# Layer 0 of a four-layer kernel: order of loads, place of the first shared block, mask comparison and expert weights

## The chip, the cores and the metric

The kernel runs on one core of a Trainium2 chip. A core has a matrix engine (TensorE, PE), three engines for element work (VectorE or DVE, ScalarE or ACT, GpSimd or POOL) and a sequencer for transfers (SyncE, SP); its transfers share 16 DMA engines. Each engine works through its own list of instructions in a fixed order and waits on semaphores for the others. The metric is the device time of one execution in microseconds (us); lower is better.

## The reference

Input is x (2 x 1024 x 256, float32; here 2048 tokens of 256 channels), a condition vector for each of the two sequences, a mask of 1024 x 1024 and the weights of four layers. Each layer adds the output of a conditioning block and a feed-forward block to x. Only layer 0 and one check for layer 1 matter here:

```python
x = x + L0_ffn(L0_cond(x, cond, weight), ...)      # layer 0
x = x + L1_ffn(L1_cond(x, cond, mask, ...), ...)   # layer 1
...
# L0_ffn
shared_out = silu(x @ sgw) * (x @ suw) @ sdw        # 256 -> 512 -> 256, every token
logits = x @ gate_w                                 # 32 experts
topk_ids, topk_val = argmax(logits), max(logits)
xs = x * sigmoid(topk_val)
# each token through the 256 -> 512 -> 256 gated block of its own expert
routed_out = (silu(xs @ g[e]) * (xs @ u[e])) @ d[e]
return shared_out + routed_out
```

The conditioning block of layer 0 multiplies x by a 256 x 256 weight, scaled for each sequence by the condition vector and normalised. Layer 1 masks its attention scores with the mask. The kernel has a short form of layer 1 for a mask whose rows are all equal, and a long one otherwise; it counts at run time the entries in which rows differ from the first.

## The kernel before

**Layout.** Tokens lie on columns in `XT` (x) and `HT` (x after the conditioning), 2 x 128 channels on the partitions; 2048 tokens are NT = 16 tiles of 128 or NB = 4 blocks of TB = 512. `Xt` and `Ht` hold the same with tokens on partitions. `Ht` is part of a buffer called ACC (`Hr`, 258 wide: 256 channels and two extra columns); its last tile, `k.zero`, also serves as a source of zeros until tile 15 is written. A ring of 20 pieces of 512 KB holds weights: two pieces take the conditioning weight and its products, three are held for the shared block, and fifteen remain, which is five experts of three pieces.

**Who sets the order.** The code lists instructions; a scheduler (the Tile framework) gives each engine its order and its semaphores from data dependences, buffer reuse and its own estimates. `_behind(k, inst, ref)` adds an order without a semaphore: `inst` comes after `ref` in the list. `_after` adds a real wait. SP issues almost all loads, in order, with at most eight semaphores in turn for outstanding ones.

**The stages of `_layer0`, in the order of the profile:**

1. SP loads the condition vector (2 KB), the first half of `XT` (1 MB, issued in `tile_adaln_ffn_kernel`), the conditioning weight `W` (256 KB), the gate weight, the second half of `XT`, the three shared weights (`ring<-in_L_s`), and then writes zeros to the row buffer `xbuf` (6,063 KB) and to a part of `ybuf` (2,688 KB) from `k.zero`. A memset on DVE (L411) fills the two extra columns of all 16 tiles of ACC.
2. DVE squares `W` (L417), PE forms the norm (`pd`, L421), and for each block of tokens two products `ph` (L433); ACT scales them into `HT` (L435).
3. Router: PE forms logits from `HT` (`ps_lt`, L1200) and transposes them (`l_pl`, L1210), DVE copies them to `l_lg` and finds the maximum and its index (L177, L179).
4. `_route_static` (L509): DVE makes a one-hot table (L186) and a running sum over the tiles (sixteen additions, L518); PE adds over the tokens of a tile (`R`, L520, and L522 after the running sum, `cnt`, L525); some twenty DVE operations (L527 to L567) turn this into a row number for each token (`rows`, L557).
5. PE turns each of the 16 tiles of `HT` into token order (`ps_tm`, L354), ACT scales it by the score into `Ht` (L447), and POOL scatters it to `xbuf` (L285; 128 rows each), after the zero store has landed. Then the 16 tiles of `XT` are turned and copied by DVE into `Xt` (L453).
6. Two of the four shared blocks (`_shared`, blocks 0 and 1): four steps `f`, each with products `spg` and `spu` (L1245), silu on ACT (`ssg`, L1250), a product on DVE (`sa`, L1252) and `spo` on PE (L1255). `_shared` calls `hook` after every step and hands it the last product and the last matmul. The result is added to `Xt` (L459).
7. `_layer1_pre` (L598): loads five weights of layer 1, loads the first mask row to all partitions (`m0`) and the mask in four pieces of 256 rows (`mm`), compares and counts (`l_ne`, L620; `l_dif`, L621; the sum over partitions `pd`, L625; `l_differ`, L627), then transposes (`l_pn`, L636) and small products for layer 1 (`pt`, `pu`, `pn`). `_router_biases` adds sixteen tiny products (`pb`).
8. The slots: 24 slots of 128 rows of `xbuf`, each with rows of one to three experts. `Slots.fetch` loads `xs` (L301, which waits for every scatter), PE transposes it (`ps_cm`, L363), DVE copies it to `xsT` (L1405). `Split.slot` (L1563) forms `fpg`, silu, the transposes `fpt` of the slot before, `fpu`, the product `fa` (L1576), and `fpo`; `faT` (L1552) is DVE's half of a copy of `fpt`. The weights of an expert are loaded when the code first needs them (`weights`, L464).
9. Overflow slots under run-time branches (L491), then shared blocks 2 and 3 with the gathering of the expert outputs, then layer 1, which reads `l_differ` (L2162).

Of the kernel before, what the change touches and what calls it, by code (L numbers as in the profile page):

```python
# [8 lines left out]
F32 = mybir.dt.float32  # L9
I32 = mybir.dt.int32  # L10
U32 = mybir.dt.uint32
U8 = mybir.dt.uint8
BF16 = mybir.dt.bfloat16
AF = mybir.ActivationFunctionType
ALU = mybir.AluOpType
AX = mybir.AxisListType
# [3 lines left out]
P = 128  # L20
D = 256

DR = D + 2
S = 1024
N = 2048
NT = N // P
TB = 512
NB = N // TB
# [12 lines left out]
class Ring:  # L41


    def __init__(self, t, n):
        self.t, self.n, self.i, self.held = t, n, 0, set()
# [33 lines left out]
def _bc(ap, axis, shape):  # L79
    return ap.unsqueeze(axis).to_broadcast(shape)  # L80


def _wload(nc, t, src):
    nc.sync.dma_start(t, src.rearrange("(c p) f -> p c f", p=P))
# [184 lines left out]
class Rows:  # L269
# [30 lines left out]
    def load(self, dst, src):  # L300
        i = self.k.nc.sync.dma_start(dst, src)  # L301
        _after(self.k, i, self.new)
        self.read.append(i.ins.name)


class Lead:
# [40 lines left out]
    return k.nc.sync.dma_start(dst.rearrange("(p r) d -> p r d", p=P), _bc(k.zero[:, 0:d], 1, [P, n, d]))  # L347


def _token_major(k, psum, src, t):  # L350

    ps = psum.tile([P, 2, P], F32, name="ps_tm", tag="t", bufs=2)
    for c in range(2):
        k.nc.tensor.transpose(ps[:, c, :], src[:, c, t * P:(t + 1) * P], k.ident)  # L354
    return ps.rearrange("p c d -> p (c d)")


# [30 lines left out]
def _layer0(k):  # L388
# [6 lines left out]
    with ExitStack() as ctx:  # L395
# [6 lines left out]
        W2, Wb1 = k.ring.take().rearrange("p (n c f) -> n p c f", n=2, c=2)  # L402
        _wload(nc, W, A["L0_cond_weight"])
        gw = rp.tile([P, 2, E], F32, name="l0_gw")
        _wload(nc, gw, A["L0_gate_w"])
        _wload(nc, XT[:, :, S:N], A["xT"][:, S:N])
        hold = []
        shw = _shared_weights(k, "L0_s1", "L0_s3", "L0_s2", F, hold)
        k.x = Rows(k, xbuf, [_zero_rows(k, xbuf)])
        k.t = Rows(k, k.tbuf, [])  # L410
        nc.vector.memset(k.Hr[:, :, D:], NONE)  # L411
        _zero_rows(k, ybuf[NS * T:(NS + NOV) * T, :])
        ys = rp.tile([P, 2, 2], F32, name="l0_ys")
        nc.vector.tensor_scalar_mul(ys, k.cT, 1.0 / 16.0)
# [26 lines left out]
        m8, ixf = _top(nc, rp, lg, E, "l0")  # L441
        score = rp.tile([P, NT], F32, name="l0_score")
        nc.scalar.activation(score, m8[:, :, 0], AF.Sigmoid)
        k.x.begin()
        rows, eid, nov = _route_static(k, rp, psum, ixf, E, C, NOV, "l0")
        for t in range(NT):
            nc.scalar.activation(Ht[:, t, :], _token_major(k, psum, HT, t), AF.Copy,  # L447
                                 scale=score[:, t:t + 1])
            k.x.scatter(k.Hr[:, t, :], rows[:, t:t + 1])


        for t in range(NT):
            nc.vector.tensor_copy(Xt[:, t, :], _token_major(k, psum, XT, t))  # L453

        def shared(tb, hook=None):
            po = _shared(k, pool, psum, HT, tb, *shw, hook)
            for i in range(2):
                t = tb * 4 + i * 2
                nc.vector.tensor_tensor(Xt[:, t:t + 2, :], po[i], Xt[:, t:t + 2, :], ALU.add)  # L459

        def weights(src):
            ws = [k.ring.take().rearrange("p (c f) -> p c f", f=f) for f in (F, F, D)]
            for w, n in zip(ws, ("L0_r1", "L0_r3", "L0_r2")):
                nc.sync.dma_start(w, A[n][src].rearrange("o (c p) f -> p (o c) f", p=P))  # L464
            return ws

        for tb in range(2):
            shared(tb)
        _layer1_pre(k, k.pre, psum)
        _router_biases(k, psum)  # L470

        ws = {}
        slots = Slots(k, pool, psum)
        split = Split(k, pool, psum, slots, F)
        for i in range(NS):
            lo, cols = i * T, []
            while lo < (i + 1) * T:

                e = lo // C
                if e not in ws:  # L480
                    ws[e] = weights(slice(e, e + 1))
                n = 64 if i % 3 == 1 else 32
                cols.append((slice(lo - i * T, lo - i * T + n), ws[e]))
                lo += n
            split.slot(i, cols)
        split.finish()
        n = nc.values_load(nov[0:1, 0:1], min_val=0, max_val=NOV)

# [17 lines left out]
        c.finish()  # L506


def _route_static(k, pool, psum, ixf, E, C, nov, name):  # L509


    nc = k.nc
# [4 lines left out]
    for t in range(NT):  # L517
        nc.vector.tensor_add(cum[:, t + 1, :], cum[:, t, :], oh[:, t, :])  # L518
    R = psum.tile([P, NT, E], F32, name=name + "_R", tag="mm")
    nc.tensor.matmul(R.rearrange("p t e -> p (t e)"), k.before,  # L520
                     oh.rearrange("p t e -> p (t e)"), start=True, stop=False)
    nc.tensor.matmul(R.rearrange("p t e -> p (t e)"), k.ones,  # L522
                     cum[:, 0:NT, :].rearrange("p t e -> p (t e)"), start=False, stop=True)
    cnt = psum.tile([P, E], F32, name=name + "_cnt", tag="mm")
# [70 lines left out]
    return r.rearrange("n i p e c f -> p n i e c f"), o  # L595


def _layer1_pre(k, pp, psum):  # L598

    nc, A = k.nc, k.A  # L600
# [3 lines left out]
        _wload(nc, w[n], A["L1_W" + n])  # L604
    with ExitStack() as ctx:
        pool = ctx.enter_context(tc_pool(k, "l1pr", 1))

        m0 = pool.tile([P, S], U8, name="l1_m0")
        nc.sync.dma_start(m0, A["mask"][0:1, :].to_broadcast([P, S]))

        k.mh = pp.tile([P, TB], U8, name="l1_mh")
        for g in range(4):
            q = slice(32 * g, 32 * g + 32)
            nc.gpsimd.tensor_copy(k.mh[q, :], m0[q, (g % 2) * TB:(g % 2 + 1) * TB])
        dif = pool.tile([P, 8], F32, name="l1_dif")
        for i in range(4):
            mm = pool.tile([P, 2, S], U8, name="l1_mm", bufs=2)
            nc.sync.dma_start(mm, A["mask"][i * 256:(i + 1) * 256].rearrange("(t p) s -> p t s", p=P))
            ne = pool.tile([P, 2, S], U8, name="l1_ne", tag="l1_big")
            nc.vector.tensor_tensor(ne, mm, _bc(m0, 1, [P, 2, S]), ALU.not_equal)  # L620
            nc.vector.tensor_reduce(dif[:, 2 * i:2 * i + 2], ne, AX.X, ALU.add)  # L621
        d1 = pool.tile([P, 1], F32, name="l1_d1")
        nc.vector.tensor_reduce(d1, dif, AX.X, ALU.add)
        pd = psum.tile([P, 1], F32, name="l1_pd", tag="t", bufs=2)
        nc.tensor.matmul(pd, k.ones, d1, start=True, stop=True)  # L625
        k.differ = pp.tile([P, 1], I32, name="l1_differ")
        nc.vector.tensor_copy(k.differ, pd)  # L627

        nat = {}
        for n in ("q", "k"):  # L630
# [754 lines left out]
class Slots:  # L1385

    def __init__(self, k, pool, psum, of=None, base=0):
        self.k, self.pool, self.psum, self.of, self.base = k, pool, psum, of, base  # L1390
        self.xs, self.dst = {}, {}

    def fetch(self, i):

        if i not in self.xs:
            self.xs[i] = self.pool.tile([P, DR], F32, name="xs", bufs=4)
            self.k.x.load(self.xs[i], self.k.xbuf[i * P:(i + 1) * P, :])

    def rows(self, i, made=None):

# [122 lines left out]
class Split:  # L1523
# [42 lines left out]
    def slot(self, i, cols):  # L1566
        nc, pool = self.k.nc, self.pool
        xT = self.slots.rows(i)
        pg = self.product("fpg", xT, cols, 0)
        sg = pool.tile([P, self.F], F32, name="fsg", tag="sg")  # L1570
        nc.scalar.activation(sg, pg, AF.Silu)
        if self.old:
            aT = self.turn(self.old[1])
        pu = self.product("fpu", xT, cols, 1)
        a = pool.tile([P, self.F], F32, name="fa", tag="sa")
        nc.vector.tensor_mul(a, sg, pu)  # L1576
        if self.old:
            self.end(self.old[0], aT, self.old[2])
        self.old = i, a, cols

    def finish(self):
        i, a, cols = self.old
# [546 lines left out]
def kernel(ctx: ExitStack, tc: tile.TileContext, A, out):  # L2129
# [17 lines left out]
    k.Ht = k.Hr[:, :, 0:D]  # L2147
    k.zero = k.Hr[:, NT - 1, :]
    _consts(k)
    _wload(nc, k.XT[:, :, 0:S], A["xT"][:, 0:S])  # L2150
    dp = ctx.enter_context(tc.tile_pool(name="rows", bufs=1, space=DRAM))
    k.xbuf = dp.tile([47 * P, DR], F32, name="xbuf")

# [106 lines left out]
```

## Time and profile before

| what | us |
|---|---|
| median of 3 runs (lowest, highest) | 1567.14 (1563.42, 1574.32) |
| the profiled execution, its own time | 1562.23 |
| its span | 1560.5 |
| PE busy in the span | 1465.7 |
| DVE, ACT, POOL busy | 477.3, 303.6, 285.4 |
| first matmul starts | 9.76 |
| first scatter issued; last one issued | 56.25; 79.62 |
| first row load `xs` issued | 84.04 |
| first transpose of a slot (`ps_cm`) | 110.89 |
| first matmul of a slot (`fpg`) | 112.10 |
| last output of a slot copied (`ys`) | 273.32 |

Times inside the kernel count from the start of the span. A line of the timeline reads: start, duration, engine, source line, operation, output<-input, shape, count; in square brackets the idle time of that engine just before, and the work that ended it. "PEld" is the load of the stationary operand, which overlaps matmuls; "SPq" is SP's issue of a transfer, not the transfer. A float32 matmul of 512 columns shows as two records. The mean granted TensorE clock over the span is 0.967 of full speed. The table of stretches gives, for each, its length and the busy time of each engine with the number of instructions.

### The profile page before, as it was taken

How to read it: one execution, taken by the hardware profiler on the slowest of the kernel's cores; microseconds unless marked ns; L12 is line 12 of the kernel's file. 1: busy time of each engine (PE TensorE's matmuls, PEld its weight loads, DVE VectorE, ACT ScalarE, POOL GpSimd, SP SyncE). 2: the span in 40 equal slices, each digit the busy share in tenths (PEclk: the TensorE clock that was granted, in tenths of full speed). 3: DMA queues.
4: the chain of work that ended last, by engine and by line, in shares of the span. 5: the costliest groups of instructions: out<-in, count | busy, mean ns of one | idle time of the engine just before them, and what ended most of it. 6: DMA issues, size and time to landing. Idle time of an engine off the chain costs nothing. (4 is left out here: it accounts for less than half of the span.)

```text
span 1560.5 us, 23587 instructions
## 1 busy us (share of the span) xinstructions
PE 1465.7 (94%) x8602; PEld 1019.3 (65%) x8602; DVE 477.3 (31%) x1591; ACT 303.6 (19%) x641; POOL 285.4 (18%) x317
## 2 busy tenths in 40 slices
PE   6879999976999999999999999999999999998897
PEld 2543333433555787555599999999995558864675
DVE  3732222223411354341121111111113514456432
ACT  2312221112111212111111111111111212125222
POOL 0410000300132242023101011010110073410342
PEclk9879999987999999999999999999999999998799
DMA  9759995813211286051142434354607257672470
GB/s 249 268 187 322 342 350 191 273 57 122 75 48 55 73 275 205 28 196 48 41 138 79 175 121 150 127 181 160 207 15 258 97 187 251 214 222 70 145 248 21
DMA packets 184243, 252.48 MB, mean 162 GB/s; under 512 B 17111, under 2 KB 137823, under 8 KB 184112
## 3 DMA queue, kind: packets, MB, share of 16 engines
q1 hardware_dynamic: 164448, 210.92, 41.3%
q0 software_dynamic: 14176, 36.63, 6.5%
q10 hardware_dynamic: 5488, 3.25, 0.7%
q8 instruction: 74, 1.21, 0.3%
q14 instruction: 57, 0.47, 0.1%
HBM read 284.86 MB, written 50.76 MB: 215 GB/s over the span
## 5 line engine op out<-in xcount | busy, mean ns | idle before, releaser
L1255 PE MATMUL spo<-ring,sa 128*128 128x256 f32 x768 | 191.9, 392 | 13.8 <-DVE sa L1252 13.8
L285 POOL DMA_INDIRECT tbuf<-ys,sdst x114 | 112.2, 984 | 506.7 <-ACT ys L1517 381.9
L1255 PEld LDWEIGHTS spo<-ring,sa 128*128 128x128 f32 x768 | 140.1, 191 | 95.6 <-DVE sa L1252 75.7
L1252 DVE TENSOR_TENSOR sa<-ssg,spu 128x512 f32<-128x512 f32 x96 | 65.9, 686 | 336.7 <-PE spu L1245 329.7
L1510 DVE TENSOR_TENSOR fa<-fsg,fpu 128x512 f32<-128x512 f32 x72 | 49.5, 687 | 315.9 <-PE fpu L1505 315.9
L1505 PE MATMUL fpu<-xsT,ring 128*128 128x128 f32 x1152 | 140.4, 275 | 0.0
L1505 PE MATMUL fpg<-xsT,ring 128*128 128x128 f32 x1152 | 140.3, 275 | 0.0
L1505 PEld LDWEIGHTS fpg<-xsT,ring 128*128 128x128 f32 x1152 | 137.1, 192 | 1.8
L1505 PEld LDWEIGHTS fpu<-xsT,ring 128*128 128x128 f32 x1152 | 134.4, 192 | 0.0
L1514 PE MATMUL fpo<-ring,fa 128*128 128x256 f32 x576 | 130.3, 379 | 0.0
L1250 ACT ACTIVATE ssg<-spg 128x512 f32<-128x512 f32 x96 | 57.3, 597 | 343.2 <-PE spg L1245 333.0
L1514 PEld LDWEIGHTS fpo<-ring,fa 128*128 128x128 f32 x576 | 106.7, 190 | 13.0
L1245 PE MATMUL spg<-HT,ring 128*128 128x512 f32 x192 | 99.9, 608 | 5.3 <-PEq L491 3.1
L1245 PE MATMUL spg<-XT,ring 128*128 128x512 f32 x192 | 98.4, 604 | 4.7 <-ACT XT L911 4.7
L1245 PE MATMUL spu<-HT,ring 128*128 128x512 f32 x192 | 92.0, 600 | 0.0
L1245 PE MATMUL spu<-XT,ring 128*128 128x512 f32 x192 | 91.6, 600 | 0.0
L1481 PE MATMUL cph<-xsT,ring 128*128 128x128 f32 x624 | 83.9, 278 | 4.1 <-DMA ring<-in_L_r 1.3
L1481 PEld LDWEIGHTS cph<-xsT,ring 128*128 128x128 f32 x624 | 76.0, 192 | 8.0 <-DVE ys L1490 3.2
L1488 PE MATMUL cpo<-ring,ch 128*128 128x256 f32 x312 | 80.2, 380 | 0.8 <-ACT ch L1484 0.8
L1509 ACT ACTIVATE fsg<-fpg 128x512 f32<-128x512 f32 x72 | 43.0, 597 | 169.7 <-PE fpg L1505 169.7
L1245 PEld LDWEIGHTS spu<-XT,ring 128*128 128x128 f32 x192 | 37.0, 193 | 44.4 <-issue 43.9
L1245 PEld LDWEIGHTS spu<-HT,ring 128*128 128x128 f32 x192 | 36.7, 194 | 42.7 <-issue 42.6
(570 smaller groups left out, 1644.8 us busy)
## 6 DMA issues: line engine op xcount, KB each, us to landing
ring<-in_L_w SPq DMA_DIRECT2D x108, 1024.0 KB
ring<-in_L_r SPq DMA_DIRECT2D x96, 512.0 KB
ring<-in_L_r SPq DMA_DIRECT2D x156, 256.0 KB
xs<-xbuf SPq DMA_DIRECT2D x138, 129.0 KB
ring<-in_L_W SPq DMA_DIRECT2D x32, 512.0 KB
yt<-tbuf SPq DMA_DIRECT2D x48, 256.0 KB
xbuf<-ACC SPq DMA_DIRECT2D x1, 6063.0 KB
ring<-in_L_s SPq DMA_DIRECT2D x6, 512.0 KB
```

The source lines that it names most:

```text
L285: i = k.nc.gpsimd.indirect_dma_start(out=self.ap, out_offset=bass.IndirectOffsetOnAxis(ap=idx, axis=0), in_=rows, in_offset=None, **end)
L1245: mm = nc.tensor.matmul(ps, W[:, c, f * P:(f + 1) * P], X[:, c, cols], start=c == 0, stop=c == 1)
L1250: nc.scalar.activation(sg, pg, AF.Silu)
L1252: mul = nc.vector.tensor_mul(a, sg, pu)
L1255: mm = nc.tensor.matmul(po[g // 2][:, g % 2, :], a[:, g * P:(g + 1) * P], W2[:, f, :], start=f == 0 and g % 2 == 0, stop=f == nf - 1, skip ...
L1481: made = [nc.tensor.matmul(ph[:, f, :], R1[:, c, f * P:(f + 1) * P], xT[:, c, :], start=c == 0, stop=c == 1) for f in range(2) for c in ra ...
L1488: made = [nc.tensor.matmul(po, h[:, f, :], R2[:, f, :], start=f == 0, stop=f == 1) for f in range(2)]
L1505: made = [nc.tensor.matmul(ps[:, j, :], W[:, c, (f0 + j) * P:(f0 + j + 1) * P], xT[:, c, :], start=c == 0, stop=c == 1) for ps, W in ((pg, ...
L1509: nc.scalar.activation(sg, pg, AF.Silu)
L1510: nc.vector.tensor_mul(a[:, f0:f0 + 4, :], sg, pu)
L1514: made = [nc.tensor.matmul(po, a[:, f, :], W2[:, f, :], start=f == 0, stop=f == 4 * nh - 1) for f in range(4 * nh)]
```

## The change

Five things, all in layer 0:

- **Order of loads.** The conditioning weight is loaded first, then `XT` in four blocks of 512 tokens, then the gate weight; the shared weights follow as before. The load of the first half of `XT` leaves `tile_adaln_ffn_kernel`.
- **The memset of the extra columns** covers tiles 0 to 14 only; the last tile, the source of the zeros, has its columns set already.
- **Shared block 0 in front of the router's sums.** `_route_static`, the turning of `HT` and `XT` and the scatters are called from hooks of the shared blocks, with `_behind` on the step's last matmul: step 0 of block 0 calls the router's sums and tiles 0 to 7 of `HT`, step 1 tiles 8 to 15, steps 2 and 3 four tiles each of `XT`; each step of block 1 two more tiles of `XT`. The order in which the instructions stand now: `spg` and `spu` of step 0 come between and after the `l_pl` transposes, its `sa` stands on DVE ahead of the one-hot table, and `R` stands on PE behind its `spo`.
- **Mask rows compared within the slots.** The comparison leaves `_layer1_pre` and becomes a generator, `_mask_rows`, with eight pieces of 128 rows; slots 1, 3, ... 17 advance it. Each comparison is ordered behind the last `fa`, and the next piece is loaded into one of two buffers.
- **Expert weights ahead of rows.** The first five experts (fifteen loads of 512 KB) are issued before the slots begin, and every row load is ordered behind the last of them on SP.

```diff
         _wload(nc, W, A["L0_cond_weight"])
         gw = rp.tile([P, 2, E], F32, name="l0_gw")
+        for tb in range(NB):
+            _wload(nc, XT[:, :, tb * TB:(tb + 1) * TB], A["xT"][:, tb * TB:(tb + 1) * TB])
         _wload(nc, gw, A["L0_gate_w"])
-        _wload(nc, XT[:, :, S:N], A["xT"][:, S:N])
...
-        nc.vector.memset(k.Hr[:, :, D:], NONE)
+        nc.vector.memset(k.Hr[:, 0:NT - 1, D:], NONE)
...
-        rows, eid, nov = _route_static(k, rp, psum, ixf, E, C, NOV, "l0")
-        for t in range(NT):
-            nc.scalar.activation(Ht[:, t, :], _token_major(k, psum, HT, t), AF.Copy,
-                                 scale=score[:, t:t + 1])
-            k.x.scatter(k.Hr[:, t, :], rows[:, t:t + 1])
-        for t in range(NT):
-            nc.vector.tensor_copy(Xt[:, t, :], _token_major(k, psum, XT, t))
...
+        def stream(t, mm):
+            nc.vector.tensor_copy(Xt[:, t, :], _token_major(k, psum, XT, t, mm))
+        def lead(f, mul, mm):
+            if f == 0:
+                k.x.begin()
+                got[:] = _route_static(k, rp, psum, ixf, E, C, NOV, "l0", mm)
+            if f < 2:
+                for t in range(8 * f, 8 * f + 8):
+                    nc.scalar.activation(Ht[:, t, :], _token_major(k, psum, HT, t, mm), AF.Copy,
+                                         scale=score[:, t:t + 1])
+                    k.x.scatter(k.Hr[:, t, :], got[0][:, t:t + 1])
+            else:
+                for t in range(4 * f - 8, 4 * f - 4):
+                    stream(t, mm)
-        for tb in range(2):
-            shared(tb)
+        got = []
+        shared(0, lead)
+        rows, eid, nov = got
+        shared(1, lambda f, mul, mm: [stream(t, mm) for t in range(8 + 2 * f, 10 + 2 * f)] if f < 4 else None)
         _layer1_pre(k, k.pre, psum)
         _router_biases(k, psum)
-        ws = {}
-        slots = Slots(k, pool, psum)
+        ws = {e: weights(slice(e, e + 1)) for e in range(5)}
+        slots = Slots(k, pool, psum, ref=sent[-1])
...
+        muls = []
+        mask = _mask_rows(k, k.pre, pool, psum, muls)
         for i in range(NS):
+            if i < 18 and i % 2 == 1:
+                next(mask)
...
-            split.slot(i, cols)
+            muls.append(split.slot(i, cols))
...
+def _mask_rows(k, pp, pool, psum, muls):
+    nc, A = k.nc, k.A
+    m0 = pool.tile([P, S], U8, name="l1_m0", bufs=1)
+    nc.sync.dma_start(m0, A["mask"][0:1, :].to_broadcast([P, S]))
...
+    for i in range(8):
+        mm = pool.tile([P, S], U8, name="l1_mm", bufs=2)
+        nc.sync.dma_start(mm, A["mask"][i * P:(i + 1) * P])
+        yield
+        ne = pool.tile([P, S], U8, name="l1_ne", bufs=1)
+        _behind(k, nc.vector.tensor_tensor(ne, mm, m0, ALU.not_equal), muls[-1])
+        nc.vector.tensor_reduce(dif[:, i:i + 1], ne, AX.X, ALU.add)
+    d1 = pool.tile([P, 1], F32, name="l1_d1", bufs=1)
+    nc.vector.tensor_reduce(d1, dif, AX.X, ALU.add)
+    pd = psum.tile([P, 1], F32, name="l1_pd", tag="t", bufs=2)
+    nc.tensor.matmul(pd, k.ones, d1, start=True, stop=True)
...
+    yield
```

In `_token_major` and `_route_static` the new argument `ref` is the matmul that the transposes, and the first matmul of `R`, are ordered behind; in `Slots` it is the load that every row load is ordered behind; `sent` collects the weight loads, and `Split.slot` returns the instruction that makes `fa`.

## The prediction

> **What bounds the kernel now.** I read the shares first: TensorE (PE) is busy 1465.7 of 1560.5 us, so a gain must come from stretches where PE stands still or runs slowly. Then I cut the front of the span into windows; the columns are stretch, length, busy us of PE, of its weight loads, VectorE (DVE), ScalarE (ACT), GpSimd (POOL), then granted clock, DMA share, GB/s.
>
> ```profile
> 0.00:10.00 10.00, 0.24 (x2) 0.24 (x2) 1.83 (x12) 1.28 (x1) 2.04 (x15) 1.00 0.62 210
> ...
> 30.00:40.00 10.00, 3.94 (x10) 1.60 (x8) 8.50 (x66) 2.70 (x7) 0.00 (x0) 0.75 1.11 223
> 40.00:50.00 10.00, 6.35 (x18) 3.65 (x19) 4.45 (x14) 2.26 (x6) 0.00 (x0) 0.57 1.09 363
> ...
> 80.00:90.00 10.00, 3.86 (x13) 2.11 (x12) 2.62 (x2) 0.19 (x1) 3.03 (x5) 0.81 0.56 167
> 90.00:100.00 10.00, 9.68 (x22) 5.75 (x23) 3.35 (x5) 0.60 (x1) 0.00 (x0) 0.68 1.06 390
> ...
> 150.00:200.00 50.00, 49.03 (x450) 19.23 (x448) 11.33 (x23) 10.36 (x23) 0.00 (x0) 1.00 1.00 347
> ```
>
> Three holes lie ahead of the slots, which begin at 110.9 us; inside the slots PE is full (49.03 of 50) and DMA too (share 1.00). The timeline gives each hole its cause:
>
> ```profile
> 9.01 0.69 DVE L417 TENSOR_TENSOR ring<-ring 128x512 f32<-128x512 f32 x1 [4.22 <-DMA ring<-in_L_cond_weight]
> ...
> 43.44 0.09 DVE L411 MEMSET ACC<- 128x32 f32 x1 [4.12 <-DMA xbuf<-ACC]
> ...
> 43.65 2.07 PE L522 MATMUL l_R<-l_cum,ones 128*128 128x512 f32 x2 [3.83 <-DVE l_cum L518]
> ...
> 84.04 0.34 SPq L301 DMA_DIRECT2D xs<-xbuf  x1
> 84.47 0.38 SPq L618 DMA_DIRECT2D l_mm<-in_mask  x1
> ...
> 87.38 2.29 DVE L620 TENSOR_TENSOR l_ne<-l_mm,l_m 128x2048 uint8<-128x2048 uint8 x1 [7.43 <-DMA l_mm<-in_mask]
> ...
> 90.32 3.78 PE L1255 MATMUL spo<-ring,sa 128*128 128x256 f32 x8 [6.46 <-DVE sa L1252]
> ```
>
> (1) The first weight lands behind 1 MB of x. (2) In the router the last two additions wait on DVE behind a memset that waits for the 6 MB zero store. (3) SyncE (SP) sits in the row load L301 until all scatters have landed; the last mask rows queue behind it, DVE waits for them, and `sa` behind DVE. The last line also shows the aftermath: 3.78 us where eight such records take 1.89 (at 74.24).
>
> **What the Trainium skill says.** *TensorE: Matmul & The Clock Gate*, Part 1 (the HAM clock gate): a PE idle for a window of about 3.4 us falls to half clock and needs about as long under load to recover. The trace agrees: weight loads 0.86 us apart from 12.48 to 14.19, then 0.43; clock 0.57 in 40–50. The same page's opening table: VectorE, ScalarE and GpSimd are strict FIFOs; agrees (the 4.12 us above). *DMA: Bandwidth & Descriptors*, "Queues, rings and completion order": a ring serves its descriptors in order, and an engine takes rows of queues in turn. So row loads queue behind expert weights, while POOL's scatters share: under 364 GB/s (64–66 us) they kept being issued every 1.27 us, landing in 2.4 to 6.6.
>
> **The change, part by part.** Times are of the profiled execution, whose own time is 1562.23 us around a span of 1560.5; that is 4.9 below the median 1567.14, so the saving is taken off the median.
>
> *Loads.* The weight (0.26 MB) now leads. The windows show 0.08, 0.22, 0.22 and 0.39 MB moved in us 3–4, 4–5, 5–6, 6–7, so it is in at 4.9, and 0.8 us later announced (the old pair was in at 8.2, DVE began at 9.01): 5.7. PE starts 3.3 us sooner. The first quarter of x is in at 6.7+0.8 = 7.5, before ph starts at 8.2; later quarters follow every 1.5 us and PE needs 3.4 each. Gate and shared weights keep their place in bytes; the zero store still ends near 43.4.
>
> *Router.* l_lg was copied by 30.97; now 30.97−3.3+0.4 = 28.1, the 0.4 for the first spg matmul, put between the l_pl transposes (0.86, less 0.46 that the second pair waited anyway). Maxima and indices 4.2 → 32.3, the new `sa` 0.69 → 33.0, one-hot 1.0 and sixteen additions of 0.224 → 37.7. The memset (L411) now spares the zero row: no wait. ACT's table loads (1.28 each, one more than before) end by 30, ahead of `sa`. PE has spg and spu done at 30.1, so still 3 us idle, where it had been at work on little from 30.2 to 45.6.
>
> *PE from 33.05 on*, at full clock: shared block 0's first spo 1.7; R and cnt 1.8; 32 token transposes (now all here) at 0.215 = 6.9; its other three steps at 5.16 (eight 512-wide matmul records of 0.43, plus spo 1.72) = 15.5; block 1 20.6. Sum 46.5 → 79.6. To it: waiting for the sums (37.7 against 36.3 reached) or cold clock, 2.5 (bounds 1.4 and 3.4); ACT and DVE hand-overs 1.5 (0 to 4; not shown before, bounded by the two table loads, 2.6, and two row-copy pairs, 1.5). Block 1 ends at 83.6. Then the layer-1 preparation: its four transpose pairs, formerly partly inside block 1, now all follow. From the old chain (natq 0.37, pt 1.05, pu 1.04, pn 0.6, pb 0.7) plus 1.3 for Xt's last adds: 7.3 → 90.9. The slots start **20.0 us sooner** (110.9−90.9).
>
> *Rows and weights.* Rows were written 9.6 us after R, 1.7 of it waiting for `spu`; now R ends 38.6 (41 if cold) and rows are there at 46.6–49. All sixteen scatters took 24.3 us; 8 of 16 Ht rows are ready, the rest by 52. Last issue 72–75, landing 75–79. SP's list: five layer-1 weights, sim, gates, then fifteen expert loads (7.9 MB) ahead of the first xs. They start near 49.6, when the ybuf zeroes land, and at 300 GB/s beside the scatters are in by 76–80; eight outstanding loads let the last be issued near 66. So xs goes out at about 77 and is in by 81–83: hidden, with 8 us to spare, behind block 1. If that cover is gone, the slots wait for xs. m0, the first mask row and POOL's four copies follow, off the path.
>
> *Mask rows within the slots.* Eight pairs of 128x1024 operations; half of 2.28 and 2.27, so 2.3 us a pair, between a slot's `fa` and the next DVE work. `faT` comes 3.5 us after `fa` (130.39 to 133.90): hidden. But in two places of the order an xsT follows (263.49, 1.5 us after `fa`): 0.9 + 1.3 us, the second with d1, pd and differ. Cost **2.2 us** (0 to 5). The loads add 6×0.13 MB in the slots, 2.3 us at 347 GB/s. Before, the last expert weights were in by about 257 and used at 263.97, so 7 us of lead remain: hidden. SP waits for DVE before each further mask row; at those places it had been waiting for PE to free the ring (31.5 us in 14 waits on ps_cm alone), so I count nothing (to 4 us).
>
> Sum: −20.0 + 2.2 = −17.8; I take **−17.5**, so 1567.1−17.5 = **1550** on the median (1544.7 for a profile like this one). Bounds of the terms: front 2.7 to 3.8, clock and hand-overs −4 to +2.5, slots −5 to 0: 12 to 22 saved.
>
> **Rivals.**
> *Rows late.* Scatters share DMA with 7.9 MB now instead of five loads; paced at 2.1 us rather than 1.5 they end at 49+34 = 83, land at 88 and xs at 92 or later; at 2.5 us, 99. For it: single scatters took 2.84 and 2.40 under load. Against: the others did not. Saved 20−8−2 = 10: 1557. Chance 0.18.
> *The slots become transfer-bound.* DMA is at 1.00; if SP's six waits for DVE cost 2 us each of issue time, plus 2.3, the 7 us of lead are gone and the end slips by 7. Against: waits for the ring, not for DMA, fill SP's list. Saved 11: 1556. Chance 0.14.
> *Slower: mask rows arrive late in the slots.* A mask row queues behind up to seven weights (7×0.52 MB at 347 GB/s = 10.6 us), and DVE, in order, holds faT and xsT behind it. One is hidden up to 1.2 us late. It eats the whole 20 us only from 3.7 us late at each of eight; 1% slower needs 5.7. At 6 us each: 8×4.8 = 38, against 20: 1585. Against: each row is asked for some four slots (26 us) ahead of its comparison in the instruction order. Chance 0.05.
> *The change does not do what it says* (the scheduler leaves the order): excluded, since in the built order R stands behind block 0's first spo and fifteen weights ahead of xs.
>
> **How the numbers follow.** My forecast has 0.63: 1545–1555. With the two rivals on the same side, 12 to 5 saved, and part of the late tail, the range is 1544 to 1562. One per cent, 15.7 us, is about what a measurement of this kernel can tell from no change. The forecast lies just beyond it: of its 0.63 I give 0.55 to a saving above 15.7, and a little (0.03) for gains that the rivals leave; within 1%: 0.08 + 0.26 + 0.03 = 0.37; slower 0.05.
>
> **What would show it.** Right: L422 near 5.7; no wait in front of the memset; rows by 49; first slot matmul at 92 (112.1 before); no DVE wait for l_mm; slots as long as before (162 us, +2). Wrong: PE waiting for xs near 90; PE waiting for ring loads late in the slots; xsT behind l_ne by more than 1.5 us; cold clock over more than 4 us after 33.

## The result and the profile after

| | before | changed |
|---|---|---|
| median of 20 runs (lowest, highest), us | 1570.36 (1563.42, 1574.32) | 1576.06 (1569.74, 1584.26) |
| ratio, 95% interval | | 1.0039 (1.0024 to 1.0054) |
| the profiled execution; its span | 1562.23; 1560.5 | 1569.74; 1567.9 |
| first scatter; last one | 56.25; 79.62 | 51.86; 70.99 |
| first row load `xs` issued | 84.04 | 77.08 |
| second shared block ends (last `spo`) | 106.3 | 100.7 |
| first matmul of a slot | 112.10 | 109.89 |
| slots: from there to the end of the last `ys` | 161.6 | 167.0 |

The change costs 0.4% where 1.1% of gain was forecast. Both profiles are quick executions: the changed kernel's is the quickest of its twenty runs, and that of before, which isn't one of the twenty, lies 1.2 us below the quickest of them and 8.1 below their median.

I matched the same instruction in both traces and took the difference of its start. The last scaling into `HT` stands at +0.1 us (later), the first scatter at −4.4, the first slot at −2.2, the last `ys` at +3.2, the end of layer 0 at +4.6. Through layers 1 and 2 that stays 4.3 to 5.2; in layer 3, 7.4 are added near 1265 us and most of them given back by 1467. So the loss lies in two places of layer 0, ahead of the slots and in them, and ahead of them a gain is lost that was there at 52 us.

The stretches of the changed kernel, columns as in the prediction (length, busy us of PE, its weight loads, DVE, ACT, POOL, then clock, DMA share, GB/s), show where:

```profile
50.00:55.00 5.00, 5.00 (x25) 3.23 (x24) 1.63 (x8) 2.63 (x7) 2.53 (x3) 1.00 1.05 341
55.00:60.00 5.00, 5.00 (x26) 3.63 (x25) 1.14 (x4) 4.22 (x6) 3.78 (x5) 1.00 1.01 349
60.00:65.00 5.00, 3.11 (x11) 1.76 (x10) 1.34 (x3) 0.00 (x0) 3.78 (x5) 1.00 1.05 402
65.00:70.00 5.00, 1.76 (x9) 0.83 (x7) 0.26 (x1) 0.00 (x0) 3.78 (x5) 1.00 1.06 403
70.00:75.00 5.00, 0.00 (x0) 0.00 (x0) 0.76 (x2) 0.21 (x1) 1.65 (x2) 0.53 1.06 404
75.00:80.00 5.00, 4.26 (x8) 2.15 (x9) 1.87 (x5) 0.39 (x1) 0.00 (x0) 0.50 1.05 387
```

The hole of before at 80 to 90 us is gone and that at 30 to 50 is smaller (PE busy 16.6 of 20 us, 10.3 before). A new one has opened from 60 to 76: of the 30 us shown PE loses 10.9. No engine is busy in its place; only POOL works evenly, and DMA is full. The timeline of the changed kernel there:

```profile
63.47 1.99 PE L1285 MATMUL spo<-ring,sa 128*128 128x256 f32 x8 [1.89 <-issue]
...
65.73 1.02 PE L1275 MATMUL spg<-HT,ring 128*128 128x512 f32 x2
...
69.74 0.69 DVE L453 TENSOR_TENSOR Xt<-spo,Xt 128x512 f32<-128x512 f32 x1 [6.33 <-remote]
...
74.67 0.69 DVE L453 TENSOR_TENSOR Xt<-spo,Xt 128x512 f32<-128x512 f32 x1 [4.24 <-remote]
74.79 0.60 ACT L1280 ACTIVATE ssg<-spg 128x512 f32<-128x512 f32 x1 [15.16 <-remote]
...
75.74 0.69 PE L355 MATMUL ps_tm<-ident,XT 128*128 128x128 f32 x2 [8.98 <-DVE Xt L465]
```

`spo` is drawn as done at 65.5 and `spg` at 66.8. DVE adds the one at 69.74 and 74.67, ACT takes the other at 74.79, and PE waits for them. "remote" means that a semaphore ended the wait but no instruction shown ends just before it. The trace's list of semaphore updates names it: PE's own signal, recorded at 60.51, then 69.71, then 74.64, 74.69, 74.73 and 74.77. The matmuls whose signals came at 69.71 and 74.64 are drawn as ending at 64.60 and 65.46, so these are 5 and 9 us late. The list of updates has holes itself (1374 updates of DVE's signal for 1463 instructions that give it; every missing one would lie within 2 us after the start of an indirect DMA of POOL), but DVE's starts at 69.74 and 74.67 agree with the two that are used here. The Trainium skill (*Perfetto Trace Analysis*, "Summary: the profiler window per engine type") says that a TensorE bar closes at an estimated end and leaves the spread of the semaphore out. That agrees with this picture; whether the matmuls themselves ran late or only their signals can't be read here.

In the slots most of the loss sits between 200 and 250 us:

```profile
150.00:200.00 50.00, 48.32 (x440) 18.61 (x432) 19.99 (x29) 10.36 (x23) 0.00 (x0) 1.00 0.97 335
200.00:250.00 50.00, 45.37 (x426) 17.71 (x428) 15.59 (x27) 9.39 (x21) 0.00 (x0) 1.00 0.98 336
```

```profile
200.00:250.00 50.00, 48.71 (x451) 19.06 (x448) 11.26 (x23) 9.77 (x23) 0.00 (x0) 1.00 0.99 352
```

The first fence is the changed kernel, the second the one before from 200 to 250 us.

### The profile page after: what moved, and what is told of

Read it like the earlier page. It is cut to its first block, busy times and chain, and to the rows that moved or that the text cites. A ratio compares the mean times of both kernels' runs of the same rounds, so it can differ in the third digit from the quotient of the medians.

```text
span 1567.9 us, 23581 instructions
## 1 busy us (share of the span) xinstructions
PE 1462.2 (93%) x8599; PEld 1018.2 (65%) x8602; DVE 479.2 (31%) x1599; ACT 304.6 (19%) x642; POOL 281.2 (18%) x317
## 3 DMA queue, kind: packets, MB, share of 16 engines
q8 instruction: 74, 1.21, 0.3%
```

## The experiments

Each kernel below has several timed runs and one profile; stalls, first slots and lengths of the slots are read from that one profile.

**Theory A, the burst:** 7.9 MB of expert weights beside the scatters hold everything up. **Theory B, the order:** token transposes and scatters put into block 0's steps do. For the slots, **theory S:** the mask comparison costs them. The first four kernels undo one part of the change each, or make one part alone.

*Weights on demand*
```diff
-        ws = {e: weights(slice(e, e + 1)) for e in range(5)}
-        slots = Slots(k, pool, psum, ref=sent[-1])
+        ws = {}
+        slots = Slots(k, pool, psum)
```


> Only the fifteen expert loads go back from 'ahead of the rows' to 'as the slots ask for them' (three of them still stand ahead of the first row load). Theory A, the burst: the stall between 60 and 76 us, in which PE is busy 9 of 20 us, comes from 7.9 MB of expert weights running beside the sixteen scatters. Then it goes: the second shared block ends near 85 us (100.5 with the change), the first slot matmul comes near 95 (109.9), held there by weights that arrive only after the rows, and the time falls by 8 to 13 us against the changed kernel, to about 1565. Theory B, the order of the work itself (token transposes and scatters put into block 0's steps): the stall stays, first slot matmul near 110, time as the changed kernel's (1576) or worse.


Measured: ratio to before 1.000 (0.9988 to 1.0013). The stall is there, with three expert loads ahead instead of fifteen: 9.7 us of PE's time lost between 50 and 80 us, and first slot matmul at 107.34. Theory A has lost its main support.

*Comparison back ahead of the slots, burst kept*
```diff
+        (the block m0 ... l_differ of the kernel before, in _layer1_pre)
-        mask = _mask_rows(k, k.pre, pool, psum, muls)
-            if i < 18 and i % 2 == 1:
-                next(mask)
```


> Only the comparison of the mask rows goes back to the layer-1 preparation, ahead of the slots; the burst stays. Theory S, the comparison costs the slots: they shrink from 167.0 us (109.9 to 276.9 in the changed kernel) to the 161.6 they took before, and nothing of it returns ahead of them, since DVE has time while PE is held up: time 5 us below the changed kernel, about 1571. Rival: the slots are longer for another reason (rows or expert weights that come late): they stay at 166 to 167 us, time 1576. The stall at 60 to 76 us stays either way.


Measured: 0.9911 (0.9872 to 0.9951), a fall of 1.3% against the changed kernel, far more than expected. The slots are back at 161.6 us, as forecast. But the stall that "stays either way" is gone: 1.1 us lost, and first slot matmul at 95.60, 16.5 sooner than before. DVE had 18 us more to do in that very stretch:

```profile
60.00:65.00 5.00, 5.00 (x18) 2.83 (x18) 5.00 (x6) 1.15 (x2) 3.78 (x5) 1.00 0.94 274
65.00:70.00 5.00, 5.00 (x23) 3.29 (x22) 5.00 (x9) 0.60 (x1) 4.09 (x4) 1.00 1.06 389
70.00:75.00 5.00, 5.00 (x18) 2.81 (x17) 4.92 (x6) 0.12 (x1) 4.39 (x3) 1.00 1.05 401
75.00:80.00 5.00, 5.00 (x20) 3.20 (x19) 5.00 (x6) 0.48 (x1) 1.59 (x3) 1.00 1.07 401
```

From 65 us on DMA is as full as in the changed kernel (389 to 401 GB/s), and PE loses nothing. The burst alone is not the cause.

*Two experts ahead:* `range(5)` becomes `range(2)`.


> Two experts (six loads, 3.1 MB) ahead of the rows instead of five. Theory A: the stall shrinks with the bytes: it ends when these loads have landed, near 62 to 66 us, so 8 to 11 us of it go, and two experts are there when the slots begin: first slot matmul at 92 to 98, time 1563 to 1568, the best of the four. Theory B: as the changed kernel, 1576.


Measured: 1.0004 (0.9988 to 1.0021); 6.5 us lost, first slot at 104.08. Stalled again.

*The kernel before with the fifteen loads ahead of the rows, and nothing else*
```diff
-        ws = {}
-        slots = Slots(k, pool, psum)
+        ws = {e: weights(slice(e, e + 1)) for e in range(5)}
+        slots = Slots(k, pool, psum, ref=sent[-1])
```


> The kernel before with nothing changed but the fifteen expert loads put ahead of the first row load. Theory A: the burst now meets the scatters at 56 to 75 us there too, and PE, DVE and ACT stand still for part of it: first slot matmul 3 to 10 us later than 112.1, time 3 to 10 us above before (1573 to 1580). Theory B: no stall; rows are hidden either way, weights are in earlier, time as before or up to 5 us less (1565 to 1570).


Measured: 0.9953 (0.9934 to 0.9972): the part that I suspected is a gain by itself. Nothing lost between 50 and 80 us, first slot at 102.64.

What do the three stalled kernels (the changed one, weights on demand, two experts ahead) share that the others lack? The mask comparison is missing beside the scatters. In the kernel before (its timeline, POOL and DVE) the two meet:

```profile
58.94 0.96 POOL L285 DMA_INDIRECT xbuf<-ACC,l_rows  x1 [0.30 <-issue]
59.92 2.28 DVE L620 TENSOR_TENSOR l_ne<-l_mm,l_m 128x2048 uint8<-128x2048 uint8 x1
60.20 2.84 POOL L285 DMA_INDIRECT xbuf<-ACC,l_rows  x1 [0.30 <-ACT l_gts L667]
63.35 0.96 POOL L285 DMA_INDIRECT xbuf<-ACC,l_rows  x1 [0.30 <-ACT ssg L1250]
...
67.69 2.28 DVE L620 TENSOR_TENSOR l_ne<-l_mm,l_m 128x2048 uint8<-128x2048 uint8 x1
68.41 2.40 POOL L285 DMA_INDIRECT xbuf<-ACC,l_rows  x1 [0.30 <-issue]
71.11 0.96 POOL L285 DMA_INDIRECT xbuf<-ACC,l_rows  x1 [0.30 <-issue]
```

A scatter takes 0.96 us of POOL, but 2.84 and 2.40 where a comparison runs beside it, and ends some 0.8 to 0.9 us after the comparison. The Trainium skill (*SBUF — State Buffer*, "SBUF: two separate sides") gives a reason: DVE and GpSimd share a pair of ports as an exclusive lock, and a DVE operation with two inputs in SBUF takes it against a GpSimd operation that reads SBUF. The trace agrees: the comparison has two such inputs; beside the reduction `l_dif`, with one, scatters keep 0.96. So the comparison broke the stream of scatters into series of at most five. **Theory C, the stream:** without a break the sixteen scatters, 1.27 us apart, are what makes PE's signals late. **Rival D:** the mask rows' loads, which held up SP's list, made the difference.

*Changed kernel with byte comparisons of no use beside the scatters* (four pairs)
```diff
+        def fill(mul):
+            for i in range(2):
+                z = pool.tile([P, S], U8, name="l1_ne", bufs=1)
+                _behind(k, nc.vector.tensor_tensor(z, XT[:, 0, 0:S // 4].bitcast(U8),
+                                                   XT[:, 1, 0:S // 4].bitcast(U8), ALU.not_equal), mul)
```


> The changed kernel with four pairs of extra byte comparisons (128x1024, 1.22 us each, of XT with itself; the result is used by nothing) put on DVE behind the multiplications of the two shared blocks, where the mask comparison stood before; no load is added or moved. Theory C, the scatters' stream: with the comparison gone from there, POOL issues sixteen scatters 1.27 us apart without a pause (51.9 to 71.0), and PE's signals come late while that lasts; a byte comparison on DVE holds POOL up for 2 to 4 us (in the run with the mask ahead of the slots: scatters 2.9, 2.5 and 3.3 us apart at comparisons of 57.2, 63.5 and 71.9) and so breaks the stream. Then the stall goes though DVE has 10 us more to do: first slot matmul near 98 (109.9), time 8 to 12 us below the changed kernel's 1576, about 1566. Rival D, the mask loads: what helped was that SP's list of expert weights was held up by mask rows and their waits for DVE. Then the stall stays and DVE's added work makes it worse: 1576 to 1582.


Measured: first slot at 95.96 (109.89), 2.3 us lost instead of 10.9, by adding 10 us of work that nobody needs. In this profile rival D falls. The time follows only in part: 0.9990 (0.9969 to 1.0011). The slots took 169.0, and the profiled run (1560.48) is the second quickest of twenty, of which twelve took 1568 to 1578; whether those stalled, no trace shows.

*Changed kernel with its scatters paced*
```diff
-                    k.x.scatter(k.Hr[:, t, :], got[0][:, t:t + 1])
+                if f == 0:
+                    todo.extend(k.x.paced(k.Hr, [got[0]]))
...
+            send(2 if f == 0 else 3, mul)      # and 3 behind each mul of block 1
```


> The changed kernel with its scatters paced: two behind the first multiplication, then three behind each further one, instead of sixteen as fast as POOL issues them; the mask comparison stays in the slots, nothing is added to DVE. Theory C: the stall at 60 to 76 us goes; last scatter at 78 to 82 us, row loads at 84 to 87, first slot matmul at 95 to 98; slots 167 us as with the change; time 1562 to 1566. Rival D: pacing the scatters does nothing, or the stall moves with the burst: first slot matmul at 108 or later, 1574 to 1580.


Measured: first slot at 96.47, 2.3 us lost, 0.9971 (0.9952 to 0.9989); the profiled run (1568.34) is among the slower of its twelve. With no work added and no load moved, this is the firmer answer to rival D. The 2.3 in this kernel and the last are another thing: DVE and ACT stood behind layer 1's small loads `l_sim` and `l_gts`. The slots took 169.9, 3 more than expected.

*Changed kernel without the mask comparison* (the flag is set by a memset)


> The changed kernel without the comparison of the mask rows and without their loads (the flag that says whether rows differ is set to 0 by a memset, which is what the comparison gives for these inputs; this part of the computation is left out). It separates the two costs of moving the comparison. Theory C: block stall as in the changed kernel (first slot matmul at 108 to 110), slots back at 162 us: 5 us below the changed kernel, 1571. Rival: if the stall had to do with the mask rows' loads that follow the row loads, it is gone as well: about 1558.


Measured: stall as expected (9.9 us lost, first slot 107.84), slots 160.1; 0.9997 (0.9975 to 1.0019). The two costs of moving the comparison are separate, and this one shows the slots' share alone.

*Comparison ahead of the slots, layer 3's scatters three to a step:* `((1, 3), 4)` becomes `((1, 3), 3)`.


> The kernel with the mask comparison back ahead of the slots (1557.5, the best so far), with one more number changed: the scatters of layer 3 go out three to a step instead of four. There the profiles of five kernels of six, all but the kernel before, show PE idle for some 7 us about 12 scatters after their stream began (in the changed kernel between 1264 and 1270 us). Theory C: slower issue takes that stall away: 5 to 7 us less, about 1551. Rival: the stall there is chance or belongs to the weights loaded beside it: no change, 1557; or the rows come later and layer 3's slots start later: up to 6 us more.


Measured: 0.9952 (0.9937 to 0.9968), against 0.9911 without the edit: a miss. Between 1246 and 1299 us of before's time it lost 14.8 us where four to a step lost 7.1. There pacing cost more than a quieter stream gave; how much of it is the later rows was not separated.

*Comparison ahead, scatters paced four to a step, `l_sim` and `l_gts` loaded first*


> The kernel with the mask comparison ahead of the slots, with two more edits: scatters go out four to a shared step behind its multiplication, and layer 1's two small loads (l_sim, l_gts) are asked for ahead of its five weights, since DVE or ACT stood 3 to 6 us behind them at 52 to 59 us in several runs. Theory C: no stall at 55 to 76 us at all, last scatter by 76, first slot matmul at 92 to 95: 1553 to 1557. Rival: comparison and pacing together make the rows late (row loads after 86): slots 3 to 6 us later than with the comparison alone, 1560.


Measured: 0.9918 (0.9886 to 0.9950), 1557.18 us; 0.5 us lost, but the last scatter at 83.71 (76 expected) and first slot at 96.90 (92 to 95). The stall is gone and the rows are late; it is no better than the comparison alone.

*Comparison ahead of the slots once more*


> The kernel with the mask comparison ahead of the slots once more, since its 1557.5 rests on five runs. Theory C: 1556 to 1560, at least 10 us below before. If the five were a lucky draw: 1562 to 1565, as the kernel that shares its layer 0 and differs in layer 3's pace (1564.1) would have it.


Measured: 1556.28, ratio 0.9905 (0.9870 to 0.9939). The first value holds: some 15 us below before and 20 below the changed kernel. It beats both. This second profile of the same kernel lost 4.3 us (1.1 in the first) and began the slots at 99.91 (95.60): at 56 to 62 us DVE waited for a mask row and ACT for `l_gts`. So single profiles of one kernel differ by 4 us at the first slot.

*The kernel before without the comparison* (flag set by a memset, rows not loaded)


> The kernel before without the comparison of the mask rows and without the loads of the rows to be compared (the flag is set to 0 by a memset; this part is left out). It has neither the burst nor the moved router, only the stream of scatters that nothing on DVE breaks. Theory C: taking 18 us of work off DVE buys little or nothing, since the stall appears here too: PE idle for 8 us or more between 62 and 82, scatters 1.27 us apart, first slot matmul at 106 or later, time 1566 to 1574. Rival: the stall needs the burst or the moved steps: none here, and the 6.46 us in which PE waited for sa behind the comparison at 90 us go as well: first slot matmul at 100 to 104, time 1560 to 1564.


Measured: 1.0019 (1.0001 to 1.0038). The kernel before, with 18 us of DVE's work taken out and nothing moved, does not get faster; its stretches:

```profile
60.00:65.00 5.00, 4.87 (x24) 2.67 (x22) 3.27 (x9) 1.67 (x3) 3.78 (x5) 1.00 0.78 292
65.00:70.00 5.00, 2.83 (x10) 1.51 (x11) 1.27 (x3) 0.00 (x0) 3.78 (x5) 1.00 0.28 102
70.00:75.00 5.00, 2.77 (x7) 0.95 (x5) 0.43 (x1) 0.60 (x1) 3.78 (x5) 1.00 0.28 102
75.00:80.00 5.00, 1.72 (x4) 1.45 (x5) 0.69 (x1) 0.34 (x1) 3.42 (x6) 0.59 0.25 78
```

PE stands as in the changed kernel, 7.8 us lost, with DMA at a quarter. First slot at 114.13, later than with the comparison (112.10). This is the strongest single profile for theory C.

*Paced kernel with the comparison only where no `xsT` follows it*
```diff
+        next(mask)                              # ahead of the slots: first loads
-            if i < 18 and i % 2 == 1:
+            if i in (1, 3, 5, 7, 9, 11, 13, 17):
                 next(mask)
...
+        next(mask)                              # behind split.finish(): sum, l_pd, l_differ
```


> The paced kernel (scatters three to a step, 1566.3) with the mask comparison still in the slots, but only at places of DVE's order where no xsT follows the comparison; the sum over the rows with its matmul goes behind the last slot. Theory S, the place: what the comparison cost in the slots (9.6 us of them in the paced kernel's profile) was paid at the two places where xsT stands behind it, once as the wait and once more as half clock after it, and at a row load that came late: slots 162 to 164 us long, time 7 us below the paced kernel, 1558 to 1560. Rival: the comparison costs by its DVE time or its loads wherever it stands: slots at 168 or more, 1566.


Measured: 0.9926 (0.9908 to 0.9944), 1560.40; slots 163.7 (169.9 in the paced kernel). The work on DVE is the same and 6.2 us of the slots' length went, so that time as such is not what they cost. The edit also asks for the mask rows sooner, so the place of the comparison and the time of its loads are not told apart. 2.1 us over the 161.6 of before remain, which I didn't trace.

Still open was what of the stream does it: the instructions, the rows or the bytes. Two more, made from the stalled kernel before without the comparison; both leave out most of the rows' contents, so only layer 0 up to the slots is read, from one execution each.

*A quarter of the rows:* `k.x.scatter(k.Hr[0:32, t, :], rows[0:32, t:t + 1])`


> The kernel before without the mask comparison (which stalls between 63 and 78 us), with each of the sixteen scatters cut to the first 32 of its 128 rows: as many instructions on POOL, a quarter of the rows and of the bytes. It leaves out three quarters of the rows, so experts and all later layers work on other data; only layer 0's profile is read, up to the first slot. If the number of instructions is what counts: stall as there, 7 to 8 us of PE's time lost between 50 and 80 us. If rows or bytes count: less than 2 us lost, first slot matmul at 102 to 106 (114.1).


*A quarter of the width:* `k.Hr[:, t, 0:64]` into a dense view of `xbuf`


> The same kernel with all 128 rows in each scatter, but 64 of the 258 columns, written close together: as many instructions and rows, a quarter of the bytes. It leaves out most of what the rows hold; only layer 0's profile is read. If the rows[...] count: stall as with full rows, 7 to 8 us lost. If the bytes count: less than 2 us lost.


Measured: 11.7 and 8.3 us lost (7.8 with full rows); first slot at 121.46 and 117.34. The stretches of the kernel with a quarter of the width:

```profile
65.00:70.00 5.00, 2.73 (x15) 1.50 (x14) 1.27 (x3) 0.00 (x0) 3.78 (x5) 1.00 0.08 26
70.00:75.00 5.00, 3.99 (x10) 1.49 (x8) 0.85 (x2) 0.00 (x0) 3.78 (x5) 1.00 0.08 26
75.00:80.00 5.00, 0.00 (x0) 0.00 (x0) 0.00 (x0) 0.60 (x1) 3.66 (x5) 0.82 0.06 20
```

DMA moves 26 GB/s at a share of 0.08, and PE stands still all the same. Neither fewer bytes nor fewer rows took the stall away; of what I tried, the unbroken series of POOL's instructions is left.

All kernels with full scatters together; a series ends where two scatters are over 1.5 us apart, "lost" is 30 us less PE's busy time from 50 to 80 us:

| kernel | longest series of scatters | PE lost, us | first slot | slots, us |
|---|---|---|---|---|
| before | 5 | 0.0 | 112.10 | 161.6 |
| before, weights ahead | 5 | 0.0 | 102.64 | 161.3 |
| comparison ahead; again | 6; 9 | 1.1; 4.3 | 95.60; 99.91 | 161.6; 160.9 |
| the same, layer 3 paced | 8 | 4.0 | 99.49 | 161.0 |
| the same, paced, small loads first | 6 | 0.5 | 96.90 | 161.3 |
| changed, filler | 7 | 2.3 | 95.96 | 169.0 |
| changed, paced | 8 | 2.3 | 96.47 | 169.9 |
| changed, paced, other places | 8 | 2.6 | 98.74 | 163.7 |
| changed | 16 | 10.9 | 109.89 | 167.0 |
| weights on demand | 16 | 9.7 | 107.34 | 166.6 |
| two experts ahead | 16 | 6.5 | 104.08 | 165.6 |
| changed, no comparison | 16 | 9.9 | 107.84 | 160.1 |
| before, no comparison | 16 | 7.8 | 114.13 | 160.5 |

Not all that is lost is the stall. With the comparison ahead (all profiles but the paced one), in the filler and in the paced kernel it is waits for layer 1's small loads or a mask row at 55 to 62 us, and so are 2.7 us with weights on demand and 2.2 in the changed kernel without the comparison. That leaves 6.5 to 10.9 us for a series of sixteen. The 2.6 of the paced kernel with other places, a series of eight, is the stall on a small scale: `spg`, drawn as done at 65.35, is taken by ACT at 67.06.

## Why the prediction was wrong, step by step

**Loads: 3.3 us forecast, 1.0 and then nothing measured.** The weight was announced at 8.00, not 5.7 (9.01 before). Its 256 packets of 1 KB moved from 4.81 to 7.63 us, beside those of x from 5.5 on; my sum let it move alone from 3 us. PE then began at 8.74, 1.0 sooner than before (9.76), and the clock took that back. In the timelines of the changed kernel, then of before:

```profile
8.00 0.69 DVE L422 TENSOR_TENSOR ring<-ring 128x512 f32<-128x512 f32 x1 [3.46 <-DMA ring<-in_L_cond_weight]
...
14.88 0.34 PEld L438 LDWEIGHTS ph<-XT,ring 128*128 128x128 f32 x1 [0.52 <-issue]
15.73 0.20 PEld L438 LDWEIGHTS ph<-XT,ring 128*128 128x128 f32 x1 [0.52 <-issue]
...
16.79 0.69 ACT L440 ACTIVATE HT<-ph,l_dd 128x512 f32<-128x512 f32 x1 [1.84 <-PE ph L438]
```

```profile
14.19 0.34 PEld L433 LDWEIGHTS ph<-XT,ring 128*128 128x128 f32 x1 [0.52 <-issue]
14.79 0.19 PEld L433 LDWEIGHTS ph<-XT,ring 128*128 128x128 f32 x1 [0.26 <-issue]
```

The weight loads of `ph` stand some 0.85 us apart at half clock and 0.43 at full. The first record of full clock is at 15.73 in the changed kernel, 7.0 us after PE began, and at 14.52 before, 4.8 after. ACT only follows PE; its last scaling stands at 27.09 (27.01 before). In the kernels with this front the full clock came 4.5 to 7.8 us after PE's first matmul and the last scaling from 2.1 us sooner than before to 0.2 later. My sum had no term for that.

**Router: right in kind.** No wait in front of the memset, `R` sooner than before (42.03 against 43.65), rows at 50.80 (55.19). The forecast of 46.6 to 49 missed by the front and a cold `spo` of 3.49 us.

**PE's work from 33.05 us: the step that failed.** It is the term "ACT and DVE hand-overs 1.5 (0 to 4)". With the series of scatters whole, PE lost 10.9 us between 50 and 80 waiting for hand-overs, and the clock was at half from 70.35 to 80.59; block 1 ended at 100.7, not 83.6. (Half clock over more than 4 us after 33 was one of the signs of being wrong that the prediction had named; it had not named this cause.) With the series broken and all else as in the change block 1 ended at 86.8 and 87.3, so the rest of the sum was 3.2 to 3.7 short, 2.3 of it the waits for layer 1's small loads. I had read the comparison as a pure burden on DVE, its 6.46 us wait, and taken it out at no price. The sign of what it held up stood in my own text: "single scatters took 2.84 and 2.40 under load". These two are the scatters of 60.20 and 68.41, each beside a comparison. I put them down to DMA load, for a rival in which scatters come late. They came in time (70.99), and in one series, and the series did the harm.

**Layer-1 preparation: 7.3 forecast; 9.2 from the end of block 1 to the first slot matmul** (8.4 with the comparison ahead).

**Rows and weights: right.** Last scatter 70.99 (72 to 75 forecast), row load at 77.08 (77), rows hidden behind block 1.

**Mask rows in the slots: right mechanism, wrong size.** 2.2 forecast (0 to 5); 5.4 measured, 7.4 and 8.3 in the filler and paced kernels. As forecast, there were two places, the second with the sum; in the changed kernel's timeline:

```profile
209.24 1.22 DVE L639 TENSOR_REDUCE l_dif<-l_ne 128x1 f32<-128x1024 uint8 x1
...
210.38 0.41 DVE L1437 COPY xsT<-ps_cm 128x256 f32<-128x256 f32 x1
...
210.70 0.41 PE L366 MATMUL ps_cm<-ident,xs 128*128 128x128 f32 x2 [1.21 <-DMA xs<-xbuf]
...
224.90 0.38 PE L643 MATMUL l_pd<-l_d,ones 128*128 128x1 f32 x2 [1.58 <-DVE l_d L641]
```

`xsT` starts when the reduction ends. By the matched instructions (before against changed) these two places cost 1.0 and 3.0 us, and row loads that came late 0.9 at 190 and 0.6 at 250. In the paced kernel it is worse: PE waited 1.94 us for the row load after the first of the two places, and stood 2.10 of the four us from 211 to 215 near the second; after each the granted clock fell to half, as its stretches show (columns as above):

```profile
195.00:198.00 3.00, 1.06 (x10) 0.61 (x12) 1.87 (x4) 0.37 (x1) 0.00 (x0) 0.94 0.91 313
198.00:201.00 3.00, 3.00 (x16) 0.38 (x8) 0.26 (x1) 0.00 (x0) 0.00 (x0) 0.50 1.08 390
...
211.00:215.00 4.00, 1.90 (x24) 0.75 (x20) 2.67 (x5) 0.37 (x1) 0.00 (x0) 0.96 1.07 397
215.00:218.00 3.00, 3.00 (x18) 0.70 (x11) 0.00 (x0) 0.17 (x1) 0.00 (x0) 0.50 1.07 390
```

In the changed kernel the waits of 1.21 and 1.58 us left the clock at 1.00. The skill (*TensorE: Matmul & The Clock Gate*, "Part 1: The HAM clock gate") lets the clock fall after an idle window of about 3.4 us; here it fell after about 2 us of waiting within three or four, and the measurement decides. My sum for the slots had waits and no stretch at half clock.

**The rivals.** Rows late, transfer-bound slots, mask rows late by a queue of weights: none of them happened as priced. My slower case needed mask rows 6 us late at each of eight places; the slower result came from a stage in which I had seen only gain. **The range** (1544 to 1562, or 0.985 to 0.997 of the median it was taken from) holds the change with the series broken only where the comparison also has other places (0.9926); with the scatters paced alone, 0.9971, it is just missed. So a right term for the hand-overs would not have been enough: the cost of the mask rows was too small as well.

## What to carry to other kernels

Before taking work off an engine, look at what that work holds up on the others: here a comparison on DVE was the brake of POOL's scatters, and taking its 18 us away gained nothing (1.0019). Try spreading a long series of indirect DMAs over the steps of the work beside it; in layer 0 a series of sixteen cost 6 to 12 us and one of five to nine, the waits for small loads apart, at most 2.6, but in layer 3 the pacing that was tried cost more than it gave. When work moves into a full stage, what counts is whose input stands behind it in its engine's list.

## What the runs showed of the hardware

- In layer 0 an unbroken series of sixteen indirect scatters from GpSimd, 1.27 us apart, came with a stall in seven kernels of seven, also at a quarter of the rows (1.17 us apart) and at 26 GB/s. In the changed kernel PE's signals, and with them DVE and ACT, came up to 9 us late. With weights on demand two recorded signals of PE that follow each other are 4.90 us apart, in the changed kernel 4.93. Why is open: no run here shows by what path GpSimd's work delays them.
- In layer 2 of the same traces (`l2c_rows`) the scatters go out in pairs with 4.15 us between, and the difference to before stays constant. In layer 3 thirty-two go out, four to a step; every profile with all rows and four to a step loses 6 to 7 us about twelve scatters in, except that of the kernel before, whose thirty-two followed 1.27 us apart without a loss. So a whole series does not stall in every execution, and in layer 3 twelve were enough. That profile lay 8 us under its median, and it was the one I predicted from.
- That profile differs in one more thing: no update of a signal is missing from it (1457 of DVE's for 1456 instructions), while each of the fifteen others lacks 83 to 111 of DVE's, all of them within 2.5 us after the start of an indirect DMA of GpSimd. So a rival stands untested: that the recording of the profile has a part in the stall. Every timed run on record comes with a span and a clock from the profiler; none shows these kernels without it.
- A byte comparison with two SBUF inputs held a scatter up until 0.8 to 0.9 us after its own end; a reduction with one input held up none.
